# Layer 0's down product: five of its eleven chunks multiplied as whole numbers, and Layer 1's binding vectors fetched first

## The chip, the cores and the metric

The kernel runs on one core of a Trainium2 chip. The metric is the time of one execution on the device in microseconds, measured three times: the median is 1410.35 us (1407.18 to 1412.27). Lower is better.

A core has five engines with queues of their own, each of which works through its instructions in order: TensorE (PE in the profile, with its weight loads as PEld), VectorE (DVE), ScalarE (ACT), GpSimd (POOL) and SyncE (SP, which here only issues DMAs). Matrix products go to PSUM, everything else is in SBUF.

## The reference, cut to what matters

Four layers follow one another on x of 4 x 256 x 512 numbers; each adds an attention and an FFN of the normalized x to x. The change is in Layer 0's FFN, whose weights are 4-bit numbers with a scale and a zero point for each group of 128 rows:

```
k = jnp.arange(K)
q = qweight[k // PACK, :] >> (k % PACK * 4)[:, None] & 15
s = scales.astype(jnp.float32)
zp = (z.astype(jnp.float32) + 1.0) * s
g = k // groupsize
w = q.astype(jnp.float32) * s[g] - zp[g]
...
gate, up = x2 @ Wg, x2 @ Wu
inter = gate * jax.nn.sigmoid(gate) * up
out = (inter @ Wd).astype(jnp.float16)
```

x2 has 1024 rows of 512; `inter` has 1376 columns, which the kernel treats as 11 chunks of 128 (padded with zeros). So within one chunk of the down product, one scale belongs to each of the 512 output columns: w = (q - (z + 1)) * s, and q - (z + 1) is a whole number from -16 to 14.

Layer 1's attention multiplies values by the signs and mean sizes of a "binding" vector `bv`, and queries and keys by those of two others (`bqk` in the kernel).

## The kernel before, in words

Tokens are eight tiles of 128 (t = 0 to 7). `layer0_attention` normalizes and transposes x into `xT`, computes the attention and splits the normalized x into `hi` and `lo`, two F32R tiles whose sum is x. Beside it, DVE makes whole-number gate and up weights (`GateUp.pieces`); the first three blocks are kept as F32R, the other eight as F16 (`held`), to be widened by ACT when needed (`widen`).

`layer0_ffn` has two stages.

*Gate and up* (lines 752 to 806). 22 sums, u = 0 to 21, alternately the gate and the up of a chunk. For each group g of 128 inputs TensorE multiplies the whole-number weights by hi and lo (F32R, line 767) into one of four PSUM buffers of two banks. The scales come after: ACT scales groups 0 and 1 (line 780), DVE scales and adds groups 2 and 3 (line 782), POOL adds the two halves (`added`, line 787), ACT takes silu (line 802), DVE multiplies gate by up (line 805). The result is `hT`, chunk by chunk.

*Down* (lines 808 to 842). Each chunk's weight is built in F32: DVE shifts and masks (line 722) and multiplies by the scale (line 726), POOL subtracts scale times zero point (line 727). Three DMAs bring the packed numbers, the scales and the scaled zero points of a chunk, the last two spread over 128 partitions. TensorE then multiplies in F32 (`product`, line 735), lhsT = a tile of hT, rhs = the chunk's weight, all eight tiles in eight PSUM banks: chunks 0 to 4 for all tiles, then chunks 5 to 10 for tiles 0 to 3, and for tile 4, 5, 6, 7 in turn. `output` rounds a sum to F16 (ACT, line 731) and adds it to x (DVE, line 732). Between tiles 4 to 7 the normalization of Layer 1 runs for tiles 0 to 3 (`Layer1.norm`, `binding`), and `values_binding` computes the signs of bv between chunks 4 and 5.

The order in these two stages is written out by hand (`tc.manual_schedule` for PE, DVE, ACT and POOL). Layer 1 behind them is ordered by a scheduler, which may also move later instructions forward in a queue: eight of POOL's sums for Layer 2's weights (lines 1107 and 1111) stand in its queue right behind the last line 727. DMAs are put on SP's queue by the scheduler; each waits for what its memory held before. `layer1_weights` (line 2117) fetches Layer 1's weights after `x2.close()`, when hi and lo are no longer read; `gate_b` and `bv` go by POOL's queue.

## Time and profile before

| | us |
|---|---|
| median of three runs | 1410.35 (1407.18 to 1412.27) |
| profiled execution | 1409.99 |
| its span, first to last instruction | 1408.3 |
| gate and up, first to last matmul | 271.8 to 363.4 |
| down, first product to the last | 365.8 to 443.6 |
| first matmul of Layer 1 on TensorE (line 940) | 444.3 |
| TensorE busy in the span | 1360.0 (97%) |
| DVE, ACT, POOL busy | 897.2, 521.3, 750.8 |
| mean granted TensorE clock | 0.985 |

Times in the trace count from the first instruction. In a row of a group, "xN" is the number of instructions, then come busy us, the mean length of one in ns, and the idle time of the engine just before, with what ended it. In a timeline the columns are start, length, engine, line, operation, output <- inputs. A matmul's recorded length (0.39 us for F32R, 0.59 for a pass in F32) is longer than the distance to the next, because matmuls overlap; the distance from start to start is the rate.

### The profile page before, as it was taken

What the parts mean: (1) busy time and instruction counts of PE and PEld (TensorE: products, weight loads), DVE (VectorE), ACT (ScalarE), POOL (GpSimd) and SP (SyncE); (2) the same over time, 40 slices, a digit from 0 to 9 for tenths busy, and PEclk for the clock granted to TensorE, in tenths of its full rate; (3) what the DMA queues carried; (4) which work ended last, traced back from release to release, by engine and by line L of the source; (5) the groups of instructions that cost most, each with busy time, mean ns of one, the idle gap of its engine ahead of it and who ended that gap; (6) DMA issues with size and microseconds to landing.
All of it is one profiled execution on the core that took longest, in us unless ns stands there. A gap on an engine that the chain in (4) does not pass through costs nothing.

```text
span 1408.3 us, 20885 instructions
## 1 busy us (share of the span) xinstructions
PE 1360.0 (97%) x7332; PEld 1069.7 (76%) x7332; DVE 897.2 (64%) x2361; ACT 521.3 (37%) x1338; POOL 750.8 (53%) x772
## 2 busy tenths in 40 slices
PE   8889999899998999999999999999999999999998
PEld 7556666578545667888888888888888888877887
DVE  7677778478928249635756756565566655768654
ACT  2434335378202212332333432333333344545430
POOL 3445546467646105864777857868558675321210
PEclk9899999899999999999999999999999999999999
DMA  5021222300510021011311203212113000403001
GB/s 196 2 58 35 46 46 66 96 0 1 168 63 16 0 83 47 30 46 35 98 46 64 68 16 94 68 46 64 53 61 105 19 27 1 135 0 113 1 1 61
DMA packets 51033, 76.54 MB, mean 54 GB/s; under 512 B 16506, under 2 KB 23829, under 8 KB 50544
## 3 DMA queue, kind: packets, MB, share of 16 engines
q1 hardware_dynamic: 50000, 74.16, 17.1%
q8 instruction: 58, 0.95, 0.3%
q10 hardware_dynamic: 816, 0.79, 0.2%
q14 instruction: 47, 0.39, 0.1%
q0 software_dynamic: 112, 0.26, 0.1%
HBM read 67.28 MB, written 7.91 MB: 53 GB/s over the span
## 4 chain that ended last, share of the span: by engine, by line
PE 85%; DVE 10%; ACT 2%; issue 2%; POOL 1%; DMA 1%; SPq 0%; DVEq 0%; ACTq 0%; POOLq 0%
PE m L1379 18%; PE m L1343 15%; PE dn L735 5%; PE gu L767 5%; PE s L1735 4%; PE av L1808 4%; PE half L282 4%; PE m L1365 3%; PE m L1355 3%; PE s L1739 2%; PE l1o L1016 2%; PE av L1809 2%; PE st L439 2%; DVE masked L393 2%; PE half L322 2%
## 5 line engine op out<-in xcount | busy, mean ns | idle before, releaser
L1783 POOL TENSOR_TENSOR p<-p,rs 128x512 f32<-128x512 f32 (+1 forms) x128 | 107.0, 857 | 149.5 <-DVE rs L1780 138.2
L1769 ACT ACTIVATE p<-p,nm 128x256 f32<-128x256 f32 (+1 forms) x256 | 113.3, 443 | 107.5 <-DVE nm L1753 107.2
L1437 DVE TENSOR_TENSOR x_sb<-x_sb,m 128x512 f32<-128x512 f32 x82 | 55.9, 685 | 82.4 <-PE m L1379 67.4
L1343 PE MATMUL m<-xT,wq_b 128*128 128x256 f32 x448 | 103.9, 380 | 3.6 <-DVE x_sb L1603 2.2
L1753 DVE CUSTOM_DVE_ANT_0 p<-s,cmask 128x256 f32<-128x256 f32 (+1 forms) x256 | 76.1, 353 | 47.5 <-PE s L1735 45.5
L1403 POOL TENSOR_TENSOR q<-q,t 128x512 f32<-128x512 f32 x64 | 82.2, 1286 | 31.5 <-DVE t L1394 28.2
L393 DVE CUSTOM_DVE_ANT_0 masked<-s,cmask 128x256 f32<-128x256 f32 (+1 forms) x256 | 89.8, 351 | 11.2 <-PE s L380 1.6
L1817 ACT COPY o<-av 128x512 f32<-128x512 f32 x64 | 37.5, 586 | 157.2 <-PE av L1809 157.2
L1326 POOL TENSOR_TENSOR c<-c,z 128x512 f32<-128x512 f32 x28 | 36.4, 1300 | 105.9 <-DVE c L1323 49.3
L1343 PEld LDWEIGHTS m<-xT,wq_b 128*128 128x128 f32 x448 | 82.1, 190 | 14.0 <-DVE x_sb L1603 2.6
L453 POOL TENSOR_SCALAR_AFFINE_SELECT keys<-keys 128x256 f32<-128x256 f32 x128 | 56.7, 454 | 65.1 <-ACT keys L449 63.7
L1379 PE MATMUL m<-wo_b,o 128*128 128x256 f32 x384 | 89.6, 379 | 0.0
L1394 DVE TENSOR_TENSOR t<-m,rope_sb 64x512 f32<-64x512 f32 (+1 forms) x144 | 86.2, 599 | 2.0
L449 ACT ACTIVATE keys<-st 128x384 f32<-128x384 f32 x128 | 57.3, 488 | 77.0 <-PE st L439 77.0
L1801 ACT COPY q<-pT 128x512 f32<-128x512 f32 x64 | 37.5, 585 | 122.6 <-PE pT L1792 120.6
L735 PE MATMUL dn<-wd,hT 128*128 128x512 f32 x176 | 76.4, 593 | 2.3 <-DVE sb L782 2.3
L787 POOL TENSOR_TENSOR sa<-sa,sb 128x1024 f32<-128x1024 f32 x22 | 62.0, 2823 | 30.5 <-DVE sb L782 30.5
L1343 PE MATMUL m<-x_s,wq_t 128*128 128x256 f32 x320 | 77.1, 386 | 1.1 <-ACT kv L1428 1.1
L1379 PEld LDWEIGHTS m<-wo_b,o 128*128 128x128 f32 x384 | 71.3, 190 | 8.8
L1343 PEld LDWEIGHTS m<-x_s,wq_t 128*128 128x128 f32 x320 | 60.8, 193 | 10.5 <-ACT kv L1428 1.5
L1808 PE MATMUL av<-q,kv 128*128 128x512 f32 x128 | 65.5, 593 | 0.6 <-ACT q L1802 0.6
L1735 PE MATMUL s<-kv,q 128*128 128x256 f32 x256 | 65.8, 379 | 0.0
(333 smaller groups left out, 3442.3 us busy)
## 6 DMA issues: line engine op xcount, KB each, us to landing
wq_b<-in_wq SPq DMA_DIRECT2D x38, 256.0 KB, 3.0
wo_b<-in_wo SPq DMA_DIRECT2D x32, 256.0 KB, 2.6
raw<-in_wo SPq DMA_DIRECT2D x16, 512.0 KB, 3.6
wkv_b<-in_wkv SPq DMA_DIRECT2D x16, 256.0 KB, 2.8
wos_d<-wos_row SPq DMA_DIRECT2D x28, 128.0 KB, 2.8
gate_q<-in_gate_q SPq DMA_DIRECT2D x11, 256.0 KB
up_q<-in_up_q SPq DMA_DIRECT2D x11, 256.0 KB
wq3s_b<-in_wq SPq DMA_DIRECT2D x8, 256.0 KB, 3.2
```

Source lines behind the costliest of these rows:

```text
L393: nc.vector.tensor_tensor_reduce(out=ap.tile([P, T], F32, tag="masked", name="masked", bufs=1)[:, 0:n], in0=self.s[part][i][:, e, :], in1= ...
L735: nc.tensor.matmul(po, lhsT=hT[:, k, t * P : (t + 1) * P], rhs=wd[:, k, :], start=k == 0, stop=k == NBLK - 1,)
L767: nc.tensor.matmul(p[:, half], lhsT=w[:, g, :], rhs=x[half][:, g], start=k == 0, stop=k == 1,)
L1343: nc.tensor.matmul(out[:, i, :], lhsT=b[:, c, i * P : (i + 1) * P], rhs=a[:, c, :], start=start and i == 0 and c == 0, stop=i == 1 and c == 1,
L1379: nc.tensor.matmul(out[:, t, :], lhsT=a[:, c, t * P : (t + 1) * P], rhs=b[:, c, :], start=start and t == 0 and c == 0, stop=t == 1 and c = ...
L1394: nc.vector.tensor_tensor(t2[at], src[of], sin[of], ALU.mult)
L1403: after(1 + 2 * pause, lambda: nc.gpsimd.tensor_tensor(dst, dst, t2, ALU.add))
L1735: nc.tensor.matmul(s1[:, i, :], lhsT=q[:, i, P:T], rhs=kt[:, 0, :], start=True, stop=True)
L1753: nc.vector.tensor_tensor_reduce(out=x[f"p{part}"][:, e, :], in0=x[f"s{part}"][:, e, :], in1=cmask if part else cmask[:, P : 2 * P], scale ...
L1769: nc.scalar.activation(p, p, AF.Exp, bias=x["nm"][:, part, e : e + 1], scale=-1.0, accum_out=x["sums"][:, part, e : e + 1],)
L1783: nc.gpsimd.tensor_tensor(p, p, bc(x["rs"][:, part, :], 2, n), ALU.mult)
L1808: nc.tensor.matmul(av, lhsT=v[:, 0:P], rhs=x["q0"], start=True, stop=False)
```

## The change

It does these things:

- Chunks 0 to 4 (`WHOLE = 5`) of the down product are multiplied as whole numbers: `whole` takes the whole-number weight q - (z + 1) of 128 output columns as lhsT (F32R) and the halves of hT (`split`: ACT copies the rounded part, POOL subtracts to get the rest) as rhs. The result is transposed: 128 output columns by 1024 tokens, in two banks.
- `scaled` scales each such block by its columns' scales, which are now one number for each partition (`gu.ds`), and adds it up in SBUF (`acc`, in the memory of the widened gate/up weights): chunk 0 by ACT and DVE in turn, later chunks by DVE, except for column block 3 of chunks 1 to 3, which ACT scales and POOL adds.
- `turned_back` brings the sum to the tokens' side: for each tile four F32 matmuls of 128x128 by the identity, added in PSUM to the F32 products of chunks 5 to 10.
- In the order, the four products of chunk 5 for tiles 0 to 3 come first; then 20 blocks of `whole`, each but every fifth followed by one F32 product (`between`), and the work of the other engines beside them (`side`). PSUM is four double banks throughout (A to D); the blocks take turns in two of them while tiles 0 to 3 fill the other two.
- The zero points of all chunks come as one DMA (F16, 11 x 512 numbers to each of 128 partitions), the scales of chunks 5 to 10 one by one. DVE subtracts the zero point instead of multiplying by the scale; POOL multiplies by the scale, and only for chunks 5 to 10.
- Building moves: chunk 5 at u = 14, chunk 0 at u = 18, chunks 6 and 1 right after the first four products, the others inside the loop. Chunks 0 and 1 are split at u = 20 and 21.
- `values_binding` comes after the outputs of tiles 0 to 3. SP fetches bqk and bv first of Layer 1's weights; bv is no longer on POOL's queue.
- In the order as built, the eight POOL sums for Layer 2 now stand between Layer 1's mask selections, and DVE's three `gather` additions before tile 7's output.

```diff
-    def layer0_attention(hook, aside, xp, wd):
+    def layer0_attention(hook, aside, xp, wdp):
...
-            self.down_zp = dram.tile([NBLK, C], F32, name="down_zp")
+            self.down_z1 = dram.tile([NBLK, C], F16, name="down_z1")
+            self.wide = held.tile([P, NBLK - READY, 2, 4, P], F16, name="gu_h")
...
             def down_weights(m):
 
-                q, s, zp = fetched_down[m]
+                w, q = wds[m], packed[m]
                 nc.vector.tensor_scalar(
                     q, q, gu.shift, 15, ALU.logical_shift_right, ALU.bitwise_and
                 )
-                w = wd[:, m, :]
-                nc.vector.tensor_tensor(w, q, s, ALU.mult)
-                nc.gpsimd.tensor_tensor(w, w, zp, ALU.subtract)
+                nc.vector.tensor_tensor(w, q, points[:, m, :], ALU.subtract)
+                if m >= WHOLE:
+                    nc.gpsimd.tensor_tensor(w, w, scales[m - WHOLE], ALU.mult)
+                elif m + 2 < WHOLE:
+                    down_fetch(m + 2)
+            def split(k, eng):
...
+                hs = [hT[:, k, h * 512 : (h + 1) * 512] for h in range(2)]
+                for i, h in enumerate(hs):
+                    nc.scalar.copy(x[2 * i], h)
+                for i, h in enumerate(hs):
+                    eng.tensor_tensor(x[2 * i + 1], h, x[2 * i].bitcast(F32), ALU.subtract)
+                halves[k] = x[:2], x[2:]
+            def whole(k, n, p):
+                for h in range(2):
+                    for i, x in enumerate(halves[k][h]):
+                        nc.tensor.matmul(
+                            p[:, h],
+                            lhsT=wds[k][:, n * P : (n + 1) * P],
+                            rhs=x,
+                            start=i == 0,
+                            stop=i == 1,
+                        )
+            def scaled(k, n, p):
+                s, a = gu.ds[:, n, k : k + 1], acc[:, n]
+                if k == 0 and n % 2 == 0:
+                    nc.scalar.activation(a, p, AF.Copy, scale=s)
+                elif k == 0:
+                    nc.vector.tensor_scalar(a, p, s, None, ALU.mult)
+                elif n == 3 and k + 1 < WHOLE:
+                    part = once.tile([P, 2, 512], F32, tag="part", name=f"part_{k}")
+                    nc.scalar.activation(part, p, AF.Copy, scale=s)
+                    nc.gpsimd.tensor_tensor(a, a, part, ALU.add)
+                else:
+                    nc.vector.scalar_tensor_tensor(a, p, s, a, ALU.mult, ALU.add)
+            def turned_back(t, po):
+                for n in range(4):
+                    nc.tensor.matmul(
+                        po[:, n * P : (n + 1) * P],
+                        lhsT=acc[:, n, t // 4, t % 4 * P : (t % 4 + 1) * P],
+                        rhs=ident,
+                        start=False,
+                        stop=n == 3,
+                    )
...
+                    if u in (14, 18):
+                        down_weights({14: 5, 18: 0}[u])
+                    if u in (20, 21):
+                        split(u - 20, nc.gpsimd)
+                side = {
+                    1: [lambda: down_weights(7), lambda: split(2, nc.gpsimd)],
+                    2: [lambda: finish(len(subs) + 1)],
+                    3: [lambda: down_weights(2)],
+                    4: [lambda: split(3, nc.gpsimd)],
+                    5: [lambda: down_weights(8)],
+                    7: [lambda: down_weights(3), lambda: split(4, nc.gpsimd)],
+                    9: [lambda: down_weights(9)],
+                    11: [lambda: down_weights(4)],
+                    13: [lambda: down_weights(10)],
+                }
...
+                for _ in range(4):
+                    t, k = between.pop(0)
+                    product(t, po[t], k)
+                finish(len(subs))
+                down_weights(6)
+                down_weights(1)
+                ring = turn[0] + 1
+                for i in range(4 * WHOLE):
+                    k, n = divmod(i, 4)
+                    p = ps("ABCD"[(ring + i % 2) % 4], [P, 2, 512], f"dw_{k}_{n}")
+                    whole(k, n, p)
+                    scaled(k, n, p)
+                    for f in side.get(i, ()):
+                        f()
+                    if i % 5 != 1:
+                        t, j = between.pop(0)
+                        product(t, po[t], j)
+                for t, k in between:
+                    product(t, po[t], k)
             x2.close()
-            ctx0.enter_context(psum_banks("ps_f1", F=4, G=4))
             l1 = layer1_begun()
...
+            for t in range(4):
+                turned_back(t, po[t])
+                output(t, po[t])
             l1.values_binding()
...
             for t in range(4, NT):
                 steps[t - 4]()
-                for k in rest:
+                for k in range(WHOLE, NBLK):
                     product(t, po[t], k)
+                turned_back(t, po[t])
                 output(t, po[t])
...
     def layer1_weights(pool):
-        w = {n: load(pool, n) for n in ("w1", "rank", "bqk")}
+        w = {"bqk": load(pool, "bqk")}
+        w["bv"] = pool.tile([P, L1_HEADS, P], F32, name="bv")
+        nc.sync.dma_start(out=w["bv"], in_=bc(d["bv"], 0, P))
+        w.update({n: load(pool, n) for n in ("w1", "rank")})
...
-        w["bv"] = pool.tile([P, L1_HEADS, P], F32, name="bv")
-        nc.gpsimd.dma_start(out=w["bv"], in_=bc(d["bv"], 0, P))
```

`finish(u)` is the part of the gate/up loop that adds, takes silu and multiplies, as a function: POOL adds sum u - 1, ACT takes silu of sum u - 2 where u is even, DVE multiplies by sum u - 2 where u is odd. In the loop it is called for each u; `finish(22)` comes after the first four products, `finish(23)` in the third step of the loop.

## The prediction

> **What bounds the kernel now.** I read the page first, then the stage with the table of windows, then the chain and single rows. Page: TensorE is busy for 97% of the span and holds most of the chain.
>
> ```profile
> PE 1360.0 (97%) x7332; PEld 1069.7 (76%) x7332; DVE 897.2 (64%) x2361; ACT 521.3 (37%) x1338; POOL 750.8 (53%) x772
> PE 85%; DVE 10%; ACT 2%; issue 2%; POOL 1%; DMA 1%; SPq 0%; DVEq 0%; ACTq 0%; POOLq 0%
> ```
>
> By windows (PE, PEld, DVE, ACT, POOL busy us, then granted clock and DMA), the two stages that are edited:
>
> ```profile
> 345.00:363.40 18.40, 18.40 (x80) 14.38 (x78) 16.82 (x17) 12.78 (x13) 13.82 (x6) 1.00 0.15 37
> 363.40:444.30 80.90, 77.91 (x196) 35.25 (x195) 47.72 (x72) 8.71 (x14) 41.98 (x31) 1.00 0.29 93
> ```
>
> The down product (363.4 to 444.3) is 78 us of TensorE in 80.9; DVE (48) and POOL (42) have room. In the end of the gate/up stage DVE (16.8 of 18.4) and POOL have little. The chain shows the same: whole stretches of one engine.
>
> ```profile
> 284.14 65.34 PE gu L767 x280
> 365.84 60.35 PE dn L735 x140
> ```
>
> **The sum without waits.** From the page's costliest groups, and from the timeline (start, length, what):
>
> ```profile
> L735 PE MATMUL dn<-wd,hT 128*128 128x512 f32 x176 | 76.4, 593 | 2.3 <-DVE sb L782 2.3
> ...
> 346.04 0.39 PE L767 MATMUL gu<-x_hi,up_w 128*128 128x512 f32 x1
> 346.27 0.39 PE L767 MATMUL gu<-x_lo,up_w 128*128 128x512 f32 x1
> ...
> 469.77 0.39 PE L1038 MATMUL l1o<-val,a 128*128 128x128 f32 x2
> 470.00 0.39 PE L1030 MATMUL l1o<-val,a 128*128 128x128 f32 x2
> ```
>
> An F32 product is two records (176 for 11 chunks x 8 tiles); inside the stage their weight loads start each 0.429 us, so a product is 0.858 us. An F32R matmul of the same shape is one record, and the next starts 0.233 later. An F32 matmul of 128x128 is two records, 0.222 from pair to pair.
> Removed: 5 chunks x 8 tiles x 0.858 = 34.3. Added: 5 chunks x 4 column blocks x 4 F32R matmuls x 0.233 = 18.7, and 8 tiles x 4 turns of the scaled sum x 0.222 = 7.1. The gap before the first product (2.3 us, until DVE has freed the PSUM pool) goes, since banks now pass on one by one. TensorE: -34.3 + 18.7 + 7.1 - 2.3 = **-10.8 us**.
>
> **What comes on DVE and POOL, and the lock.** The order as built has on POOL, after the last two gate/up sums: split of chunk 0 (2 instructions), add 20, split of chunk 1 (2), add 21, and only then the scaling of chunk 6. TensorE's order is four products of chunk 5, one block of chunk 0 (4 F32R), and then a product of chunk 6, which waits for that scaling; everything on TensorE is behind it. So the question is when POOL gets there. In the trace DVE's two-input instructions and POOL's exclude one another:
>
> ```profile
> 356.41 5.75 POOL L787 TENSOR_TENSOR sa<-sa,sb 128x1024 f32<-128x1024 f32 x2
> 357.57 2.32 DVE L805 TENSOR_TENSOR hT<-hT,sa 128x1024 f32<-128x1024 f32 x1
> 372.85 1.43 POOL L727 TENSOR_TENSOR wd<-wd,xT 128x512 f32<-128x512 f32 x1 [1.28 <-DVE wd L726]
> 373.20 1.63 DVE L726 TENSOR_TENSOR wd<-xT 128x512 f32<-128x512 int32 x1
> ```
>
> L805 takes 1.22 alone and 2.32 here, until the first add is over; L726 takes 0.69 alone, 1.63 behind a POOL instruction. The rows of L782 (PSUM in, 1.27 us) never stretch. The Trainium skill (SBUF — State Buffer, section "SBUF: two separate sides") has the rule: DVE and GpSimd share a port pair, an exclusive lock for a whole instruction, and the loser fully blocks. It speaks against this change: running side by side, POOL's queue at the wait below is 11.2 us; by the lock DVE's instructions are added to it (14.0). The rows say that the rule holds for these very instructions, so I take the lock.
>
> *Gate/up stage.* Building chunk 5 at block 14 is what chunk 0 was at 18: nothing new. Chunk 0 at 18 now has no POOL step, but its DVE subtraction meets add 18 (ready at 353.98) and waits to 356.7, so DVE is 2 us behind; the ring of four banks has 1.1 of slack. TensorE ends at 364.4 rather than 363.4: **+1.0** (0 if the subtraction comes first).
>
> *First wait.* Add 19 ends at 363.3 (behind the hT product of 359.7). From there POOL: 4 x 1.28 (splits) + 2 x 2.40 (adds) + 1.28 (scaling) = 11.2; DVE instructions that take turns with it: hT product 1.20, shift 0.48, subtraction 0.69, shift 0.48 = 2.85. End: 363.3 + 14.0 = 377.3. TensorE is there at 364.4 + 4 x 0.858 + 0.93 = 368.8. **+8.6**; without the lock add 19 ends at 361.0 and the scaling at 372.2, against 367.8: +4.4, the low end. ACT's silu of chunk 10 waits for add 20 as well, and the first evacuation of the loop stands behind it (until about 370); it is not needed before 377.
>
> *Clock.* Such a hole is new. The trace has a thinner one at 450 to 456 (PE busy 1.60, 1.21, 0.48 of 2 us) and after it
>
> ```profile
> 456.00:458.00 2.00, 1.60 (x10) 1.48 (x11) 2.00 (x4) 0.76 (x2) 2.00 (x3) 0.88 0.00 0
> 458.00:460.00 2.00, 2.00 (x7) 1.48 (x6) 1.22 (x3) 0.98 (x2) 2.00 (x5) 0.50 0.00 0
> ```
>
> clock 0.50. The skill (TensorE: Matmul & The Clock Gate, "Part 1: The HAM clock gate"): an idle window of about 3.4 us halves the clock, a busy one restores it. By the rows alone nothing says when it comes back; by the rule 3.4 us at half are **+1.7**. Ends 0 and 3.4.
>
> *Second wait, the ring of two.* From 377.3, TensorE has 1 + 15 products and 19 blocks: 16 x 0.858 + 19 x 0.933 = 31.5 us. A block can't start until the one two before it is evacuated. DVE in that time: 13 accumulations (as L782, 1.20 start to start), 2 scalings from PSUM (1.2, twice L98's 0.68 less its overhead), one hT product 1.2, seven pairs shift and subtraction at 1.13: 27.1. POOL has 4 scalings, 6 split steps and 3 adds (4 x 1.28 + 6 x 1.28 + 3 x 2.40 = 20.0) there, so most subtractions wait as at 373.20: 7 x 0.94 = 6.6, and the shifts too, by about half of that, 3.2 (estimate from the same row). 36.9 - 31.5: **+5.4**. Low end 0.5 (DVE 27.1 fits, single lags of a bank stay); high end 7.5, if POOL is always first.
>
> *Turned-back sums, outputs.* Four products (3.4) cover the last evacuation. The value vector's seven DVE steps (about 3.7) now lie ahead of the norm of tiles 0 to 3; those, four statistics (3.2), root and two normalizations (1.7) end about 10 us after the outputs; TensorE needs them after two tiles, 2 x (6 x 0.858 + 0.89) = 12.1. Hidden, by 2 us. **0**.
>
> *DMAs.* bv leaves POOL's queue (0.54 us of issue) for SP's, second of Layer 1's, which wait until the last block has read x_hi. It took 4.1 us to land and is needed 3.4 + 3.6 + 1.3 = 8.3 later: hidden. The next, w1 (6.8 us to land), is needed some 28 us later. SP also holds Layer 2's eight blocks (issued at 392 to 396 before) until this memory is free, so their eight POOL sums (10.1 us, done at 396 to 408 before) come between Layer 1's mask selections. POOL has 13.27 us idle there before 476.7, and the first masks are read at 468.6, three sums later than 458.6: 463.3. Hidden. 33 fetches (7 MB) become 18 (5 MB). The zero points are one transfer of 1.44 MB, ahead of the last up_q, which was issued at 260.0 and read at 267.7. At w_sb's rate (1 MB in 6.8 us) 9.6 us; at the page's best slice (196 GB/s) 7.3: up_q may be 2 to 4 us late. DVE has 1.92 us idle just behind. 0 to 2, taken **+0.3**.
>
> Sum: -10.8 + 1.0 + 8.6 + 1.7 + 5.4 + 0.3 = **+6.2**. The profiled execution took 1409.99 (span 1408.3, 1.7 around it): 1416.2. The median of the three runs is 0.36 above it: **1416.5 us**.
>
> **Rivals.**
> *The lock costs half* (DVE's queue slips in between, POOL's order runs through): -10.8 + 0.5 + 5.5 + 1.7 + 1.5 = -1.6, 1408.7, no change that counts. For it: the shifts of L722 (0.47 to 0.48) never stretched. Against it: there POOL was idle when they began; now it has a queue of its own.
> *The other side: the scaling of chunk 6 is in time.* One mechanism: POOL passes the adds at 2.40 with no DVE between them and the clock doesn't fall: -10.8 + 4.4 + 0.5 = -5.9, 1404.4. It decides from a first wait of 6.1 us or less, with a second of 0.5 (-10.8 + 6.1 + 0.5 = -4.2, which is 0.3%). Against it: even undisturbed, the scaling ends 4.4 us after TensorE asks for it, and 1.7 more would do.
> *Transfers and clock add up*: zero points late and the clock halved twice, +6.2 + 2 + 3.4 = +11.6, 1422.
> *No effect at all*: the order shows that TensorE's work does fall, so only balance can give it.
>
> **How the numbers follow.** Likeliest 0.52 (1413.5 to 1420); half lock 0.27; other side 0.12; adding up 0.09. Within 0.3% (4.2 us, about what this kernel's runs can tell from no change) are the half lock and about 0.04 of the likeliest: same 0.31; slower 0.48 + 0.09 = 0.57; faster 0.12. Range 1405 to 1422, in the likeliest case alone 1413.5 to 1420.
>
> **What would show it.** Of the changed kernel: "dw" at 0.233 us a matmul and the turns at 0.22; in the first microseconds after the last "gu", one hole of 5 to 9 us on TensorE before a "dn", ended by POOL's scaling (the step that I trust most); clock 0.5 after it; in the loop waits of "dw" for DVE of 1 to 2 us; DVE's subtractions and shifts stretched to about 1.6 and 1 us. I am wrong if the hole is under 4 us, if POOL's splits run side by side with DVE, or if a wait on a transfer stands in Layer 1.

## The result, and the profile after

The changed kernel takes 1419.01 us (median of nine runs, 1411.43 to 1420.54) against 1407.18 us of the one before (nine runs as well, the three of the table above among them): 1.0070 times, with a 95% interval of 1.0052 to 1.0088. It is slower, by 0.7%. Measured again beside other kernels (run "again" below) it was 1415.38 us, 1.0055 (1.0037 to 1.0074). The profiled execution has a span of 1418.6 us, 10.3 more than before.

The page of the changed kernel, in the two lines that answer to those of before (busy time by engine; the chain by engine):

```profile
PE 1359.8 (96%) x7396; PEld 1079.5 (76%) x7396; DVE 918.4 (65%) x2377; ACT 531.7 (37%) x1353; POOL 764.2 (54%) x779
PE 83%; DVE 12%; ACT 2%; issue 2%; DMA 1%; POOL 1%; DVEq 0%; ACTq 0%; POOLq 0%
```

TensorE's work is shorter, but its recorded busy time is the same, and DVE holds more of the chain. (A matmul at half clock counts as busy for longer: 0.63 us instead of 0.40 in the rows below.) The two edited stages by windows, last part of gate/up and then the whole down product (PE, PEld, DVE, ACT, POOL busy us, granted clock, DMA):

```profile
348.17:366.57 18.40, 17.92 (x76) 13.79 (x76) 17.06 (x15) 13.83 (x15) 14.18 (x7) 1.00 0.06 15
366.57:456.25 89.68, 76.01 (x260) 44.38 (x258) 65.87 (x87) 17.88 (x27) 44.20 (x29) 0.92 0.12 28
```

The down product takes 89.7 us, 8.9 more than before the change (363.52 to 444.29: 80.8), though TensorE has 11.3 us less to do in it. DVE has gone from 48 to 66 us, POOL from 42 to 44, the clock from 1.00 to 0.92. Four names are used from here on. A *hole* is a time in which TensorE waits. The *ring* is the pair of double banks in which the blocks of `whole` take turns. The *root* is ACT's root of the variances of Layer 1's norm (L129). *rank* is the matmul with which Layer 1's own products begin on TensorE (L1048). What TensorE waited for, from 363 to 457 us (total, times, longest; the four that matter):

```profile
PE dn L799 <- POOL wd L743: 6.6, 1, 6.6
PE dn L799 <- ACT o L795: 3.0, 1, 3.0
PE dw L772 <- DVE gu_h L791: 2.1, 4, 0.8
PE dn L810 <- ACT o L795: 1.4, 2, 0.7
```

The first is the wait that the prediction put in the middle of its sum, the third is its wait for the ring. The second and the fourth it had at nothing. The rows themselves, and the clock around the first hole, in windows of 3.41 us (why this length, the last section shows):

```profile
377.64 2.08 PE L799 MATMUL dn<-wd,hT 128*128 128x512 f32 x2 [6.56 <-POOL wd L743]
379.94 0.63 PE L772 MATMUL dw<-h_up,wd 128*128 128x512 f32 x1
384.64 0.40 PE L772 MATMUL dw<-h_gate,wd 128*128 128x512 f32 x1
420.61 2.05 PE L810 MATMUL dn<-ident,gu_h 128*128 128x128 f32 x16 [0.68 <-ACT o L795]
433.67 7.11 PE L799 MATMUL dn<-wd,hT 128*128 128x512 f32 x12 [3.01 <-ACT o L795]
442.38 5.32 PE L799 MATMUL dn<-wd,hT 128*128 128x512 f32 x12
```

```profile
370.06:373.47 3.41, 1.02 (x5) 0.50 (x3) 3.38 (x3) 3.11 (x4) 3.41 (x2) 1.00 0.00 0
373.47:376.89 3.42, 0.00 (x0) 0.00 (x0) 3.39 (x3) 0.00 (x0) 3.42 (x3) 0.50 0.00 0
376.89:380.30 3.41, 2.66 (x4) 1.51 (x5) 1.24 (x1) 0.00 (x0) 0.69 (x1) 0.50 0.12 43
380.30:383.71 3.41, 3.41 (x8) 2.34 (x7) 2.21 (x3) 0.54 (x1) 0.00 (x0) 0.50 0.12 34
383.71:387.13 3.42, 3.42 (x13) 2.26 (x12) 3.11 (x4) 1.60 (x3) 3.19 (x2) 1.00 0.00 0
```

Behind the hole an F32R matmul takes 0.43 us from start to start instead of 0.233, until 383.7. Behind the second hole, at 433.67, six products take 7.11 us instead of 5.32.

Totals of one kernel lie up to 14 us apart. So the experiments are read by three stretches of each profile as well: gate/up (first matmul of L846 to the first product), blocks (to the first turned-back sum), output (to the first matmul of "rank"). The changed kernel's two profiles agree in all three to 0.01 us. The last column compares with runs of the kernel before that were taken beside those of the row.

| run | gate/up | blocks | output | sum | median us | against before (95%) |
|---|---|---|---|---|---|---|
| before | 94.1 | 78.4 (all of down) | | 172.5 | 1407.2 | |
| changed | 93.05 | 52.31 | 37.37 | 182.73 | 1419.0 | 1.0070 (1.0052 to 1.0088) |
| again | 93.04 | 52.31 | 37.37 | 182.72 | 1415.4 | 1.0055 (1.0037 to 1.0074) |
| early6 | 93.03 | 48.44 | 35.68 | 177.15 | 1411.8 | 1.0027 (1.0014 to 1.0039) |
| outs | 94.58 | 52.42 | 30.60 | 177.60 | 1408.9 | 1.0009 (0.9994 to 1.0025) |
| stats | 94.58 | 52.52 | 33.27 | 180.37 | 1411.8 | 1.0037 (1.0021 to 1.0053) |
| both | 93.03 | 47.94 | 30.59 | 171.56 | 1407.9 | 0.9995 (0.9975 to 1.0015) |
| both_oldbv | 93.04 | 49.38 | 30.60 | 173.02 | 1404.9 | 0.9984 (0.9968 to 1.0000) |
| both_dve | 93.04 | 50.97 | 30.60 | 174.61 | 1406.2 | 0.9988 (0.9971 to 1.0005) |
| spread | 97.46 | 44.52 | 30.60 | 172.58 | 1407.2 | 0.9988 (0.9967 to 1.0009) |
| relief | 93.03 | 48.66 | 30.60 | 172.29 | 1406.6 | 0.9987 (0.9972 to 1.0001) |
| four | 93.06 | 45.45 | 34.03 | 172.54 | 1408.4 | 0.9998 (0.9983 to 1.0013) |
| relief_nopart | 93.04 | 47.23 | 30.60 | 170.87 | 1402.6 | 0.9977 (0.9958 to 0.9996) |
| shifted | 93.03 | 45.61 | 30.60 | 169.24 | 1403.5 | 0.9965 (0.9945 to 0.9984) |

The 94.1 of before hold the gap of 2.3 us ahead of its first product. Bare TensorE time of the changed kernel would be 24 x 0.858 + 20 x 0.933 = 39.3 us in "blocks". In "output" it would be 30.2 us: 24 x 0.858 for the products, 8 x 0.89 for the turned-back sums, and 2.5 for what the kernel before has there too, two transposes and `alpha` of Layer 1 and the last wait for ACT.

The 94.58 of two profiles has a half-clock window (0.96 over 260 to 300 us) at its start. In "blocks" the stretches of half clock differ: none in both_dve, four and relief_nopart, one of 3.4 us in both, both_oldbv, spread, relief and shifted, two in early6, more in the others. One costs about 1.7 us if TensorE has work throughout it. Two kernels with the same order there (both, both_oldbv), each with one such stretch but not at the same place, differ by 1.4 us; a difference of that size alone shows no effect.

### The profile page after: what moved, and what is told of

Same layout as the page of the kernel before. It is cut to its first block, busy times and chain, and to the rows that moved or that the text cites. A ratio compares the mean times of both kernels' runs of the same rounds, so it can differ in the third digit from the quotient of the medians.

```text
span 1418.6 us, 21042 instructions
## 1 busy us (share of the span) xinstructions
PE 1359.8 (96%) x7396; PEld 1079.5 (76%) x7396; DVE 918.4 (65%) x2377; ACT 531.7 (37%) x1353; POOL 764.2 (54%) x779
## 4 chain that ended last, share of the span: by engine, by line
PE 83%; DVE 12%; ACT 2%; issue 2%; DMA 1%; POOL 1%; DVEq 0%; ACTq 0%; POOLq 0%
PE m L1487 18%; PE m L1451 15%; PE gu L846 5%; PE s L1843 4%; PE av L1916 4%; PE m L1473 3%; PE m L1463 3%; PE half L283 3%; PE st L440 2%; PE dn L799 2%; PE s L1847 2%; PE av L1917 2%; PE l1o L1124 2%; DVE masked L394 2%; PE half L323 2%
## 5 line engine op out<-in xcount | busy, mean ns | idle before, releaser
L1511 POOL TENSOR_TENSOR q<-q,t 128x512 f32<-128x512 f32 x64 | 82.0, 1283 | 31.5 <-DVE t L1502 28.2
L1925 ACT COPY o<-av 128x512 f32<-128x512 f32 x64 | 37.4, 585 | 157.2 <-PE av L1917 157.2
L1909 ACT COPY q<-pT 128x512 f32<-128x512 f32 x64 | 37.4, 585 | 122.1 <-PE pT L1900 122.0
L1487 PE MATMUL m<-wo_t,o_s 128*128 128x256 f32 x256 | 59.2, 379 | 0.0
```

The source lines that it names most:

```text
L1487: nc.tensor.matmul(out[:, t, :], lhsT=a[:, c, t * P : (t + 1) * P], rhs=b[:, c, :], start=start and t == 0 and c == 0, stop=t == 1 and c = ...
L1511: after(1 + 2 * pause, lambda: nc.gpsimd.tensor_tensor(dst, dst, t2, ALU.add))
```

## Experiments

**The changed kernel once more (again).**

> The changed kernel itself, as it is, run beside the other kernels of this group so that they have it on the same chip. From its own runs so far (1411 to 1420.5 us) the median is expected at 1416 to 1419 us, and the length from the first gate/up matmul to the first rank matmul at 182 to 183 us, as in its first profile.

Median 1415.4 us, 0.6 under what was expected; length 182.72 us, as expected.

**Chunk 6 built earlier (early6).** Is the hole a matter of POOL's order?

```diff
-                    if u in (20, 21):
-                        split(u - 20, nc.gpsimd)
+                    if u == 20:
+                        split(0, nc.gpsimd)
+                    elif u == 21:
+                        down_weights(6)
...
-                down_weights(6)
+                split(1, nc.gpsimd)
                 down_weights(1)
```

> Of the changed kernel only the place of two pieces of POOL's and DVE's work is altered: the weights of chunk 6 are built behind block 21 (where the split of chunk 1 was), and the split of chunk 1 comes where they were, behind the last gate/up sum. Order theory: the hole before the first product of chunk 6 (6.6 us in the changed kernel) is a matter of POOL's order; it shrinks to 0 to 1.5 us, about 1.5 us of wait appear ahead of chunk 1's first block, the clock stays at 1.00 behind it (2.6 us), rank starts about 7 us earlier than in the changed kernel, and the time is about 1412 us. Rival (amount): the same instructions have to pass the port that DVE and POOL share before chunk 1 can go on, so the hole only moves into the ring of two banks; the gain is 3 us or less, the time 1416 or more.

Total 1411.8 us, as the order theory had it, but the detail is half a miss. TensorE of early6:

```profile
372.48 2.08 PE L799 MATMUL dn<-wd,hT 128*128 128x512 f32 x2 [2.51 <-POOL wd L743]
385.27 0.51 PE L772 MATMUL dw<-x_hi,wd 128*128 128x512 f32 x1 [2.09 <-DVE gu_h L791]
```

The hole is 2.5 us, not 0 to 1.5, the clock still halves behind it, and a wait of 2.1 us on the ring of two is new. "Blocks" lost 3.9 us, not 7; the further 1.7 in "output" are the clock, which here stayed at 1.00 behind the unchanged wait of 3.0 us. That the total came out right is therefore in part luck. And part of the rival holds: some of the hole moved into the ring.

**Tiles reordered in the output stage (outs), and the value vector behind the statistics (stats).** What makes the stage 37.4 us instead of 30.2?

```diff
-            for t in range(4):
+            for t in (0, 2, 1, 3):
                 turned_back(t, po[t])
                 output(t, po[t])
...
-            for t in range(4, NT):
-                steps[t - 4]()
+            for i, t in enumerate((4, 6, 5, 7)):
+                steps[i]()
```

> Of the changed kernel only the order of the token tiles in the last stage is altered: sums are turned back and put out in the order 0, 2, 1, 3, then 4, 6, 5, 7, so that two tiles that share one PSUM tile are never next to each other. Sharing theory: the stage from the first turned-back sum to the first rank matmul (37.4 us in the changed kernel) is long because a tile's products wait for ACT to have read its neighbour in the same PSUM tile (0.7 + 0.8 + 3.0 us, and 1.9 us of half clock behind the longest); it falls by 6 to 7 us, to 31 us, and the time is about 1412 us. Rival (vector theory): the wait is for the root behind the seven steps of the value vector, which the order of the tiles doesn't touch; then tile 6's turned normal forms wait in its place, the stage falls by 2.5 us at most, and the time is 1416.5 or more.

```diff
-            l1.values_binding()
...
                     mom.update(moments(range(t0, t0 + 4)))
+                    if half == 0:
+                        self.values_binding()
```

> Of the changed kernel only one thing is altered: the seven DVE steps of the value vector come behind the four statistics and the root of tiles 0 to 3, no longer ahead of them. Both theories of the output stage expect the 3.0 us wait of tile 5 to fall to about 0.7 us (ACT's root no longer stands late in front of tile 4's output) and the clock to stay at 1.00 behind it (1.9 us): 4 us less, 1415 us. If tile 5's wait stays at 3.0 us, the value vector has no part in it.

"Output" of outs is 30.60 us, every wait but the last gone; the sharing theory's 31 holds, the vector theory's 34.9 doesn't. That of stats is 33.27, 4.1 less, as expected. (The times, 1408.9 and 1411.8 us, are both 3 us under the expected ones.) TensorE in outs (two rows) and in stats (one row):

```profile
421.22 3.78 PE L810 MATMUL dn<-ident,gu_h 128*128 128x128 f32 x32
431.02 5.40 PE L799 MATMUL dn<-wd,hT 128*128 128x512 f32 x12
```

```profile
428.55 5.42 PE L799 MATMUL dn<-wd,hT 128*128 128x512 f32 x12 [0.61 <-ACT o L795]
```

Both causes are therefore links of one chain, and ACT and DVE of the changed kernel show it:

```profile
425.75 0.68 DVE L980 TENSOR_REDUCE alpha_v<-bv 128x4 f32<-128x512 f32 x1
429.52 0.69 DVE L126 BATCH_NORM_STATS2 st<-x_sb 128x6 f32<-128x512 f32 x1
432.84 0.30 ACT L129 ACTIVATE rstd<-mv,eps 128x4 f32<-128x4 f32 x1 [6.32 <-DVE mv L127]
433.05 0.57 ACT L795 CAST o<-dn 128x512 f16<-128x512 f32 x1
```

The value vector delays the statistics by 3.8 us; ACT waits at the root (L129) for them; tile 4's output stands behind the root in ACT's queue; and tile 5's products wait for that output, because tiles 4 and 5 are now halves of one PSUM tile.

**Both together (both), and with the old fetches (both_oldbv).**

> The alterations of early6 and of the tile order together. If the hole and the output stage are independent losses, their gains add up: about 13 to 14 us less than the changed kernel, 1405 us, rank starts near 443 us, and the kernel is level with the one before or up to 0.3% faster. If the amount of work on DVE and POOL is what sets the end (rival), the sum is 1411 or more.

The sum of the stretches fell by 11.2 us, to 171.56, not by 13 to 14: "output" gave all of its 6.8 us, "blocks" 4.4. At 1407.9 us the kernel is level with the one before. That lies between the two theories. The gains of the single runs (3.9 in "blocks", 6.8 in "output") add up within the 1.4 us named above, so the two losses are independent of each other; but what is left in "blocks", 47.9 us against 39.3 of bare work, does not go with the order alone.

```diff
-        w = {"bqk": load(pool, "bqk")}
-        w["bv"] = pool.tile([P, L1_HEADS, P], F32, name="bv")
-        nc.sync.dma_start(out=w["bv"], in_=bc(d["bv"], 0, P))
-        w.update({n: load(pool, n) for n in ("w1", "rank")})
+        w = {n: load(pool, n) for n in ("w1", "rank", "bqk")}
...
+        w["bv"] = pool.tile([P, L1_HEADS, P], F32, name="bv")
+        nc.gpsimd.dma_start(out=w["bv"], in_=bc(d["bv"], 0, P))
```

> The kernel with chunk 6 built earlier and the tiles reordered, with the last part of the change undone: the binding vectors of Layer 1 are fetched as before the change (bqk third on SyncE's queue, bv last on POOL's). If fetching them first is worth nothing, as forecast, the stage from the first turned-back sum to the first rank matmul stays at 30.6 us within 0.5 us and the time within 2 us. If it was needed, the value vector's first DVE step waits for bv, and with it the statistics, tile 5's root and the turned normal forms: the stage grows by 2 us or more.

"Output" is 30.60 against 30.59 us. Fetching the binding vectors first is worth nothing here. The time missed its 2 us (1404.9 against 1407.9), on another chip and with intervals that overlap; "output", which is where the vectors are used, is the surer sign.

**Where the building is done (spread; tiles as in outs), and who splits (both_dve).**

```diff
-                    if u in (14, 18):
-                        down_weights({14: 5, 18: 0}[u])
+                    if u in {4: 5, 6: 0, 8: 6, 10: 1, 12: 7, 14: 8}:
+                        down_weights({4: 5, 6: 0, 8: 6, 10: 1, 12: 7, 14: 8}[u])
...
-                down_weights(6)
-                down_weights(1)
...
-                    1: [lambda: down_weights(7), lambda: split(2, nc.gpsimd)],
+                    1: [lambda: split(2, nc.gpsimd)],
...
-                    5: [lambda: down_weights(8)],
```

> The changed kernel with the tiles reordered, and with the building of chunks 5, 0, 6, 1, 7 and 8 spread over the gate/up stage (behind blocks 4, 6, 8, 10, 12, 14) instead of 5 and 0 there (14, 18) and the others in the down loop. Place theory: DVE and POOL have room in the gate/up stage (about 12 and 18 of 60 us idle) and none around its end, so the first hole goes (0 to 0.5 us), the clock stays, the ring of two waits for under 1.5 us, and from the last gate/up matmul to the turned-back sums it is 40 to 42 us (48 with chunk 6 early, 52 in the changed kernel; 24 x 0.858 + 20 x 0.933 = 39.3 bare); time about 1400 to 1402 us. Rival: each chunk built there makes TensorE wait for DVE's sums through the lock, 1 us or more each, and gate/up grows by 4 to 6 us, which takes the gain.

The first hole is gone and "blocks" fell to 44.5 us (40 to 42 were expected; one wait of 2.3 us for the ring is left), but gate/up grew by 4.4: the rival. DVE's two rows for chunks 5 and 0 show the two prices that a chunk has there, beside POOL idle and behind POOL's sum:

```profile
297.08 0.69 DVE L741 TENSOR_TENSOR wd<-wd,xT 128x512 f32<-128x512 int32 x1
305.34 2.79 DVE L741 TENSOR_TENSOR wd<-dq,xT 128x512 fp32r<-128x512 int32 x1
```

> The kernel with chunk 6 built earlier and the tiles reordered, and the splits of chunks 1 to 4 (eight subtractions of 128x512) moved from POOL to DVE. Lock theory (a two-input instruction of POOL shuts DVE's out for its whole length): a split holds the shared port for 1.28 us on POOL and about 0.69 us on DVE, so 8 x 0.6 = 4.7 us of port time go, the waits of TensorE between the last gate/up matmul and the turned-back sums (8.6 us above the bare products with the clock) fall by 2 to 4 us. Rival (DVE is full of its own work, and POOL's instructions lie beside it): DVE gets 8 x 0.69 = 5.5 us more in the loop in which the ring of two already waits for it, and these waits grow by 2 to 5 us.

(In both_dve, `split(k, nc.gpsimd)` reads `split(k, nc.vector)` for k = 1 to 4.) "Blocks" grew by 3.0 us against both and by 1.6 against both_oldbv, whose order is the same, and that without a stretch of half clock, while those two have one each: work taken from POOL and put on DVE makes the stretch longer. TensorE's waits for the ring went from 3.0 to 6.9 us. The lock theory's gain didn't come, and DVE was not blocked less often: its instructions with inputs in SBUF lasted 7.6 us longer in "blocks" than they do alone, against 7.3 in both and 8.8 in both_oldbv. Two of the eight moved splits were among those that lasted longer (1.6 us instead of 0.68).

**What TensorE needs first, first (relief).** Split 0, the scaling of chunk 6 and split 1 come before the last two sums on POOL; those sums and two hT products go into the loop; ACT evacuates all of chunk 0; tiles as in outs.

```diff
                     sums[u].scaled()
-                    finish(u)
+                    if u < 21:
+                        finish(u)
...
+                    elif u == 21:
+                        down_weights(6)
+                        split(1, nc.gpsimd)
...
-                finish(len(subs))
-                down_weights(6)
                 down_weights(1)
...
-                    2: [lambda: finish(len(subs) + 1)],
...
+                    4: [lambda: finish(len(subs) - 1), lambda: split(3, nc.gpsimd)],
+                    6: [lambda: finish(len(subs))],
+                    10: [lambda: finish(len(subs) + 1)],
...
-                if k == 0 and n % 2 == 0:
+                if k == 0:
```

> The changed kernel with the tiles reordered (0, 2, 1, 3, then 4, 6, 5, 7) and with the work around the end of gate/up put in the order in which TensorE needs it: on POOL split of chunk 0, scaling of chunk 6, split of chunk 1, and only later, in the loop, the last two gate/up sums; the last two products into hT also in the loop; ACT evacuates all four blocks of chunk 0 instead of two. Nothing is added or left out. If what remains (8.6 us above the bare products from the last gate/up matmul to the turned-back sums, with chunk 6 early) is work that is crowded into the first 15 us and needed there by nobody, the first hole goes (0 to 0.5 us), the clock stays at 1.00, waits of the ring are 1 to 3 us, this stretch takes 40.5 to 42.5 us instead of 47.9, from the first gate/up matmul to rank 164 to 166.5 us (172.5 before the change), and the time is 1399 to 1402 us, faster than before by 0.4 to 0.6%. Rival (DVE and POOL with their shared port are full over the whole loop): the waits move to the later blocks, the stretch takes 45 us or more, and the time is 1404 or more.

The hole is gone (no wait on POOL is left), and yet "blocks" is 48.66 us, 0.7 more than in both. TensorE of relief, and its window over the stretch:

```profile
385.88 0.50 PE L772 MATMUL dw<-x_hi,wd 128*128 128x512 f32 x1 [2.17 <-DVE gu_h L789]
391.20 0.50 PE L772 MATMUL dw<-x_hi,wd 128*128 128x512 f32 x1 [1.47 <-DVE gu_h L789]
396.63 0.50 PE L772 MATMUL dw<-x_hi,wd 128*128 128x512 f32 x1 [2.44 <-DVE gu_h L789]
```

```profile
366.94:415.60 48.66, 42.28 (x130) 24.50 (x128) 42.38 (x35) 12.37 (x16) 34.25 (x21) 0.96 0.09 17
```

All the waits are on DVE's evacuations now, further back: 6.3 us in four. DVE is busy for 42.4 of 48.7 us. Of these, 12.6 us are what its shifts and subtractions last longer than alone (0.48 and 0.69 us); each of the eleven longer ones ends 0.3 to 0.6 us behind the end of a POOL instruction. Its own work is 29.8 us, less than TensorE's 39.3. This is the rival, and a main finding: the hole was the place of the loss, and DVE beside POOL its cause, as far as these runs show. A ring of more than two double banks, in which a late evacuation would cost less, was not tried.

**Less of it: four chunks (four), no additions on POOL (relief_nopart), shifts elsewhere (shifted).**

```diff
-WHOLE = 5
+WHOLE = 4
+PLAIN = (5, 6, 7, 8, 9, 10, 4)
...
-                    if i % 5 != 1:
+                    for _ in range(1 + i % 2):
                         t, j = between.pop(0)
```

> The kernel of the last run with four chunks of the down product by whole numbers instead of five (chunk 4 is built as F32 weights with its scale), and with all 24 F32 products of tiles 0 to 3 laid between the sixteen blocks. TensorE alone: 28 x 0.858 + 16 x 0.933 = 39.0 us from the last gate/up matmul to the turned-back sums and 34.0 us from there to rank, 3.1 us more in all than with five. If the loop is full on DVE and POOL (48.7 us in the last run for 39.3 of TensorE), a chunk less takes 4 x 1.2 us of evacuations and two splits from it: that stretch takes 40 to 43 us, gate/up to rank 167 to 170 us, and the time is 1401 to 1403 us, 0.2 to 0.4% faster than before the change. Rival: the waits come from the order of the blocks, not the amount; then the stretch stays at 46 us or more, and the time is 1407 or more.

"Blocks" is 45.45 us, between the two theories (43 and 46; no stretch of half clock fell into it), and nothing is left after the 3.4 us that "output" grows by: 172.54, 1408.4 us. All five of its waits in "blocks" are for weights or an hT product that come too late for the new spacing (up to 1.8 us), so it doesn't settle what four chunks could give.

```diff
-                elif n == 3 and k + 1 < WHOLE:
+                elif False:
```

> The kernel of the last run with one thing altered: the fourth block of chunks 1 to 3 is added into its sum by DVE straight from PSUM (1.2 us each) like the others, no longer by ACT's copy and POOL's addition (2.4 us each on POOL alone, 2.4 to 3.3 in the trace). Lock theory: POOL's 3 x 2.4 us shut DVE's SBUF instructions out for about as long (two of them stretched by 2 us each in the last run), so DVE gets 3 x 1.2 = 3.6 us more and 4 us of waiting less, and the stretch from the last gate/up matmul to the turned-back sums is the same within 1 us (47.7 to 49.7). Rival (no lock, DVE's own work alone counts): it grows by 3 to 4 us, to 52.

DVE was given 3 x 1.2 = 3.6 us, POOL relieved of 7.2, and "blocks" went from 48.66 to 47.23 us. The stretch by windows:

```profile
361.33:408.56 47.23, 41.09 (x129) 23.38 (x128) 41.94 (x38) 9.13 (x13) 26.02 (x18) 1.00 0.09 17
```

DVE's busy time, blocked time included, fell from 42.38 to 41.94 us in spite of three instructions more: what its instructions last longer than alone went from 12.6 to 8.6 us. The clock fell once in relief (1.7 us lost) and not here, so the stretch is rather the same than shorter; it is 0.5 under what the lock theory had (47.7 to 49.7), and without a lock it would have grown by 3.6. That is the lock theory's case. What differs from both_dve: the work that DVE gets here reads PSUM, and none of its 16 accumulations took more than 1.28 us. The kernel is the first that is faster than the one before beyond its interval.

```diff
+                    if u in (4, 6, 8, 10, 12):
+                        unpack(u // 2 + 4)
...
+                if m <= WHOLE:
+                    unpack(m)
```

> The kernel of relief_nopart with one thing altered: the shift that unpacks the codes of chunks 6 to 10 (0.48 us of DVE each, stretched to 1.4 to 2.6 us behind POOL in the loop) is made in the gate/up stage, one behind each of the blocks 4, 6, 8, 10 and 12. If the down loop is full on DVE and the gate/up stage has gaps of about 0.5 us per block, gate/up grows by 0 to 0.7 us and the stretch from the last gate/up matmul to the turned-back sums falls by 2.4 to 4 us (47.2 before); from the first gate/up matmul to rank 167.5 to 169.5 us, and the time is 1399 to 1402 us. Rival: the gaps are not where the shifts fall, or each shift waits for POOL's sum there; gate/up grows by 2 us or more and nothing is gained (171 us or more).

Gate/up stays at 93.03 us, the sum is 169.24 as expected. "Blocks" falls by 1.6, not by 2.4 to 4; a stretch of half clock (1.7 us) fell into it and into none of relief_nopart. The time is 1403.5 us, a little above the expected 1402. It is faster than both kernels: 0.9965 of the one before (0.9945 to 0.9984). That it is faster than relief_nopart (1402.6 us, on another chip) the times do not show. DVE in its gate/up stage, a shift and what follows it:

```profile
304.82 0.47 DVE L735 TENSOR_SCALAR wd<-wd,shift_sb 128x512 int32<-128x512 int32 x1
306.04 1.28 DVE L863 SCALAR_TENSOR_TENSOR sa<-gu,gu_s,sa 128x1024 f32<-128x1024 f32 x1 [0.75 <-PE gu L848]
```

The shift takes 0.47 us, and DVE then still waits 0.75 us for TensorE: a gap that was free. In the loop of relief_nopart the shifts of chunks 6 to 8 took 0.48, 1.50 and 1.41 us.

## Why the prediction was right, and where it was not

It was right in direction and range (slower; 1416.5 us forecast, range 1405 to 1422, the likeliest case 1413.5 to 1420). The change came out larger than forecast: +6.2 us forecast, +10.3 in the profiles, +11.8 in the medians. The absolute time is nearer (1416.5 against 1419.0) by luck, as the three runs of before from which it starts have a median 3.2 us above that of all nine. The mechanism was right for the first hole; one step, taken as hidden, was wrong and made the size too low, and one term has nearly its size for another reason than the one given. Every term, from gate/up to rank in the profiles:

| step of the sum | forecast | measured | how |
|---|---|---|---|
| TensorE's work | -10.8 | -11.3 | 48 x 0.858 + 20 x 0.933 + 8 x 0.89 + 2.5 = 69.5, against 80.8 |
| gate/up stage | +1.0 | +1.3 | 93.05 against 363.52 - 271.75 = 91.77 |
| first wait | +8.6 | +6.6 | row 377.64 |
| clock behind it | +1.7 | +2.6 | 377.64 to 383.78: 6.14 for 3.58 of work (2 products, 2 blocks) |
| ring of two | +5.4 | +3.8 | 383.78 to 418.88: 35.1 for 31.3 (18 products, 17 blocks) |
| turned-back sums, outputs | 0 | +7.2 | 37.37 against 30.2 |
| zero points' DMA | +0.3 | +0.45 | gate/up starts 1.77 later, 1.32 of it from 87 us on already |
| sum | +6.2 | +10.6 | rank 444.29 to 456.25, less 1.32 |

(The 1.32 us are a lower clock between 60 and 120 us, 0.86 against 0.94, in the attention. The rest of the program, behind rank, gives back 1.6: 962.4 us against 964.0, which had a stretch of half clock at 1311 us. The 2.5 in the first row are those of "output" above.)

*Gate/up stage and zero points.* The subtraction of chunk 0 met POOL's sum as forecast (at 356.56, for 2.78 us instead of 0.69). The last up_q comes behind the zero points on SP's queue, and DVE waits for it, which it did not before:

```profile
269.83 0.49 DVE L664 TENSOR_SCALAR up_q<-up_q,shift_sb 128x512 int32<-128x512 int32 x1 [0.73 <-DMA up_q<-in_up_q]
```

The profile of before is ahead by 1.32 us until here, and by 1.77 behind it.

*First wait.* Its place, engine and queue were as forecast; POOL in the changed kernel:

```profile
361.80 3.33 POOL L866 TENSOR_TENSOR sa<-sa,sb 128x1024 f32<-128x1024 f32 x1 [3.02 <-PE gu L846]
369.90 3.65 POOL L765 TENSOR_TENSOR x_lo<-hT,x_hi 128x512 fp32r<-128x512 f32 x2
373.51 2.79 POOL L866 TENSOR_TENSOR sa<-sa,sb 128x1024 f32<-128x1024 f32 x1
376.25 1.33 POOL L743 TENSOR_TENSOR wd<-wd,xT 128x512 f32<-128x512 f32 x1
```

From the end of add 19 to that of the scaling it was 12.45 us, not 14.0: DVE's instructions got in between about once (POOL's own work there is 11.2 us), not four times as the forecast had. Reordering removed the wait, and the time came back in the ring (relief).

*Lock.* Taken as the rule, and borne out by relief_nopart; both_dve doesn't speak against it, but suggests that nothing is won by giving DVE instructions which POOL's make longer too. The Trainium skill (SBUF — State Buffer, section "SBUF: two separate sides") also counts an instruction in a two-port mode among those that are locked out; the one-input shift of 0.48 us was stretched to 1.0 to 2.6 us here, where the forecast had about 1; whether it is in such a mode no run shows.

*Clock.* It fell to half behind the hole and came back, as forecast. The term was too small because one window's length of work was taken as its price (1.7 us): in the windows above, the clock is at half for three of them, the second with work for 2.66 of 3.41 us, and comes back only behind the third, which is full of work.

*Ring of two.* The term has about its size, but not by its reason. The forecast had DVE overfull in the loop, 36.9 us for 31.5 of TensorE's, of which 9.8 were instructions lasting longer beside POOL. From 377.30 to 418.90 DVE was busy for 31.7 us, and its shifts and subtractions lasted only 3.6 us longer than alone. By the forecast's own sum that would nearly have fitted. TensorE's waits were single ones, four of 0.3 to 0.8 us between 390 and 402, where 1 to 2 us each were expected; behind that DVE waited for TensorE.

*Turned-back sums, outputs: the step that failed.* "Hidden, by 2 us" compared the normalized tiles with the turned normal forms that need them, and those were indeed in time. Not followed was ACT's queue: the root waits for the statistics, tile 4's output stands behind the root, and tile 5 needs tile 4's half of the PSUM tile free. In place of 0 it cost 7.2 us: waits of 3.0 and twice 0.7, 1.8 of half clock behind the longest (7.11 us for 5.32), and some 1 us that no single wait shows. Run outs, which only reorders the tiles, took 6.8 of them away. It also overlooked that tiles 0 and 1, 2 and 3 now share a PSUM tile (0.7 us twice, behind the last evacuation it had named). The text of the kernel shows both: `two[:, 0], two[:, 1]`, and `values_binding` ahead of `norm`.

*Hidden steps.* bv and bqk: shown to be worth nothing (both_oldbv). Layer 2's sums and the other DMAs: the waits of TensorE that the trace shows from rank to 700 us are the same in number and length as before to 0.1 us, and none is for a transfer; they were not tried by themselves. *Rivals.* None was the case. Half a lock comes near the first wait (5.5 forecast, 6.6 measured), but not the total.

## What to carry to other kernels

A change that takes work from TensorE has to be summed on the engines that take it over, with their blocked time: TensorE was relieved of 11.3 us here, and the best order found kept 3.3 (172.5 to 169.2), because DVE, lengthened by POOL beside it, was nearly full (42 of 47 us in relief_nopart). When a step is called hidden, follow each in-order queue that its result passes, and ask which instruction stands behind a waiting one; and look at what shares a buffer with what. Where the two shut each other out, taking 7.2 us from POOL cost nothing though DVE, the engine that is waited for, had to do the work in 3.6, reading PSUM; eight subtractions in SBUF moved the same way cost 1.6 to 3.0 us.

## What the hardware showed that was not expected

- Holes of TensorE much shorter than 3.4 us can halve the clock. Of eighteen holes of 1.6 to 2.7 us in "blocks" of these profiles, nine were followed by a clock of 0.50 for about 3.4 us each (1.7 us lost), which began between 0.2 us ahead of the end of the hole and 1.8 us behind it: 1.61 in outs, 1.76 in shifted, 2.15 in both_oldbv, 2.51 in both among them. Nine were not: 1.73 in both, 2.52 in both_oldbv, 2.69 in relief_nopart, 2.72 in both_dve among them.
- How the hole lies goes far to decide it. In each profile, up to its last few microseconds, the stretches of half clock last a whole number of times 3.41 us, and all changes of the clock lie whole multiples of 3.41 us apart. On this grid, the hole of 2.5 us ahead of chunk 6 in early6 (first two rows, next window at half) and in both_oldbv (last two rows, clock stays):

```profile
368.84:372.25 3.41, 1.12 (x5) 0.57 (x3) 3.34 (x5) 3.41 (x5) 1.16 (x1) 1.00 0.00 0
372.25:375.67 3.42, 3.19 (x6) 1.89 (x7) 0.72 (x1) 0.71 (x2) 3.42 (x3) 0.50 0.20 58
```

```profile
366.59:370.00 3.41, 1.87 (x7) 0.87 (x5) 3.34 (x5) 2.65 (x4) 1.13 (x2) 1.00 0.00 0
370.00:373.42 3.42, 2.44 (x9) 1.71 (x10) 1.82 (x2) 1.47 (x3) 3.42 (x2) 1.00 0.08 9
```

In early6 nearly all of it falls into one window, in which TensorE is busy for 1.12 of 3.41 us; in both_oldbv the border of two windows cuts it. From 262 to 470 us of the fourteen profiles, counted so: of windows at full clock with TensorE busy for less than 43%, all 18 were followed by half clock; with 43 to 53%, 6 of 17; with more, none of 774. This holds for these stages with their dense products; in the attention ahead of them, windows busy for up to 90% were at times followed by half clock, so recorded busy time is not the whole measure. What sets the clock within the middle group stays open. The Trainium skill (TensorE: Matmul & The Clock Gate, "Part 1: The HAM clock gate") has free-running windows of that length, after an idle one of which the clock is halved: the grid agrees, but a window need not be idle for it, as those busy for 30 to 42% show.
- The first 265 us, in which no experiment alters anything, moved the start of gate/up between 266.4 and 274.6 us from profile to profile, with the clock (0.94 to 0.98 from 120 to 265 us). The three stretches behind it repeated to 0.01 us in the two profiles of the changed kernel, and gate/up took 93.03 to 93.06 us in ten of the thirteen profiles behind the change. A gain of 3 us is read more surely from there than from totals.
